# Reciprocals spread over partitions by four transfers of 32 source partitions each, in place of sixteen of one source partition each

## The chip, the cores and the metric

The kernel runs on one core of a Trainium2 chip. The metric is the device time of one execution in microseconds, as the median of a few runs. A core has five instruction streams that work side by side and wait for each other by semaphores: PE (matrix multiplications), DVE (vector work), ACT (activations and copies), POOL (a second vector engine) and SP, which here only issues transfers (DMAs). The transfers themselves are moved by 16 DMA engines.

## The reference, cut to what matters

The input x has 32 images of 256 channels and 32 x 32 = 1024 positions. Each image is group-normalised (32 groups of 8 channels), goes through a strictly causal attention with 8 heads of 32 channels, and is added to the result:

```python
def reference(x, q_w, q_b, kv_w, kv_b):
    xf = gn(x).reshape(B, C, S)                  # B=32, C=256, S=1024
    q = einsum('oc,bcs->bos', q_w, xf) + q_b
    kv = einsum('oc,bcs->bos', kv_w, xf) + kv_b  # k, v: 256 channels each
    # 8 heads of 32 channels
    scores = einsum('bhqd,bhkd->bhqk', q, k) / sqrt(32)
    attn = softmax(where(tril(ones, -1) == 0, -10000, scores))
    attn = where(tril(ones, -1) == 0, 0, attn)
    out = einsum('bhqk,bhkd->bhqd', attn, v)
    return x + out                               # all in float32
```

## The kernel before, in words

**Tiling.** An image lies in SBUF as 128 partitions x 2 groups x 1024 positions: channel c is partition c mod 128 of group g = c // 128, so a group holds four heads (j = 0 to 3) of 32 partitions. The attention of an image is 24 steps: two groups g, two halves hf of 512 query positions, and 4 or 8 blocks k of 128 keys. A step multiplies keys with queries for four heads (line 215, tile sT), takes exponentials on ACT (line 220, tile e), masks the diagonal block on POOL (line 225), and two steps later multiplies with the values (line 243, tile acc) while DVE adds the exponentials up over the key blocks (line 248).

**Denominators.** When a pair n = 2g + hf is through, `sums` (line 260, tile pd) reduces the summed exponentials over the key partitions with a matrix that puts the sum for head j of the pair n into the partitions 32j + n, 32j + n + 4, ..., eight copies each. `den` collects the four pairs: partition p of `den` holds 512 sums of head p // 32 and pair p mod 4. `invert` (line 279) takes the reciprocals of `den` in four pieces of 128 columns, tile rec.

**Spread and finish.** The final product needs each reciprocal on all 32 partitions of its head. `spread` (line 281) does that by DMAs from rec to a tile rb of 128 x 2 x 1024, which SP issues. `finish` (line 293) is called four times per image, once per pair n: DVE multiplies the numerators with the pair's 512 columns of rb (line 297), POOL adds x (line 298) and copies the first column of x (line 300), and after each second pair SP stores a group of the image (line 302).

**What sets the order.** PE, ACT, DVE and POOL run in the order in which the code emits instructions. A table `at` says in which step what is emitted beside the attention steps: the projections of the next image (lines 176 and 191, tiles pp and ppv), the norm of the image after that (lines 135 to 163), and, four steps into the next image and later, the denominators' check, the four pieces of `invert`, then `spread`, and the four `finish` calls five to eight steps behind `spread`. SP issues its DMAs in the order of the code as well. All matmuls of the projections, the norm's matmuls (pm, pv) and pd write through one single PSUM buffer, "misc", so each waits until the one before has been read by ACT or DVE. Each DMA carries one of eight semaphore lanes in turn (DMAHW0 to DMAHW7), and a DMA whose lane is in use first waits for that lane's last DMA.

**Names.** b is the image. v (line 196) is the evacuation of ppv by DVE, rstd (lines 155 and 156) that of pv, xn (line 163) the normalised image, num (line 252) the numerators.

Of the kernel before, what the change touches and what calls it, by code (L numbers as in the profile page):

```python
# [17 lines left out]
P = 128  # L18
HD = 32
CPG = 8  # L20
HALF = 512
# [9 lines left out]
def tile_norm_attention_residual(  # L31
# [19 lines left out]
    nc = tc.nc  # L51
# [4 lines left out]
    NH = S // HALF  # L56
# [18 lines left out]
    for n in range(4):  # L75
# [5 lines left out]
        out=avg, in_=avg, pattern=[[-CPG, P // CPG], [0, CPG]],  # L81
# [3 lines left out]
        out=avg, in_=avg, pattern=[[CPG, P // CPG], [0, CPG]],  # L85
# [24 lines left out]
    def unshifted():  # L110
# [170 lines left out]
        def spread(b):  # L281
            rec = live.pop(("rec", b))
            rb = work.tile([P, NG, S], F32, tag="rb", name=f"rb_{b}")
            for j in range(4):
                for n in range(4):
                    src = rec[HD * j + n : HD * j + n + 1, :]
                    nc.sync.dma_start(  # L287
                        out=rb[HD * j : HD * (j + 1), n // NH, (n % NH) * HALF : (n % NH + 1) * HALF],
                        in_=src.unsqueeze(1).broadcast_to([1, HD, HALF]),
                    )  # L290
            live["rb", b] = rb

        def finish(b, n):
# [25 lines left out]
        for b in range(B):  # L319
            if b + 2 < B:  # L320
                when(b * N, lambda b=b: load(b + 2))
                for n, f in zip((4, 6, 10, 14, 16, 18), prepare(b + 2)):
                    when(b * N + n, f)
            if b + 1 < B:
                for n, f in enumerate(projections(b + 1)):
                    when(b * N + 2 * n + 1, f)
            for s, (g, hf, k) in enumerate(per):
                if k == (hf + 1) * BPH - 1:
                    when(b * N + s + LAG + 2 + (s + LAG) % 2, lambda b=b, g=g, hf=hf: sums(b, g, hf))
            end = (b + 1) * N + LAG + 2  # L330
            when(end, lambda b=b: check_sums(b))
            for c in range(BPH):
                when(end + 1 + c, lambda b=b, c=c: invert(b, c))
            when(end + BPH, lambda b=b: spread(b))
            for n in range(4):
                when(end + BPH + 5 + n, lambda b=b, n=n: finish(b, n))
# [174 lines left out]
```

## Time and profile before

| | us |
|---|---|
| median of 3 runs | 2982.25 (2981.96 to 2987.22) |
| profiled execution, its own time | 2987.61 |
| its span, first to last instruction | 2985.9 |
| PE busy (matmuls) | 2317.2 (78%) |
| DVE busy | 1671.4 (56%) |
| ACT busy | 1386.7 (46%) |
| POOL busy | 960.5 (32%) |
| mean granted PE clock (1 is full speed) | 0.886 |

PE, DVE, ACT and POOL work side by side, so their busy times overlap and none alone is the span. Of a group of instructions the page gives busy time, the mean of one, and the idle time of the engine just before them with what ended most of it. The chain is the work that ended last, followed back in time. A transfer has two times: how long SP was occupied with issuing it, and the time from issue to landing.

### The profile page before, as it was taken

To read this page: it belongs to the slowest core of one execution; us is meant where nothing else is said; L and a number is where in the kernel's file an instruction comes from. 1 tells how busy PE (TensorE), PEld (TensorE's weight loads), DVE (VectorE), ACT (ScalarE), POOL (GpSimd) and SP (SyncE) were. 2 spreads that over 40 slices of the span, in tenths; PEclk is the share of its full clock that TensorE was granted. 3 is DMA by queue.
4 is the path that set the end of the run, shared out by engine and by line. 5 is a ranking of instruction groups with operands and counts; after the bars stand their busy time and mean duration, and the time that the engine had idled before them with its cause. 6 is when DMAs were issued, how large, how long until landed. Compare 5 with 4: busy or idle time off the path is not lost.

```text
span 2985.9 us, 38251 instructions
## 1 busy us (share of the span) xinstructions
PE 2317.2 (78%) x15502; PEld 860.3 (29%) x15502; DVE 1671.4 (56%) x1641; ACT 1386.7 (46%) x1921; POOL 960.5 (32%) x817
## 2 busy tenths in 40 slices
PE   5977798777897777887777977778977779877762
PEld 2322232222232222332222322222322223222320
DVE  2655565455575555664555655555645556555553
ACT  2644454444554444554444544445544445444441
POOL 1332333323242323233322324232333233333242
PEclk9988898888998888998889988889988889888885
DMA  1055433454433554334554335543335543344444
GB/s 69 1 43 43 14 38 36 41 43 24 32 37 37 43 43 22 32 37 40 43 43 14 37 37 43 43 22 33 36 39 43 43 15 38 36 41 29 29 22 36
DMA packets 44183, 104.14 MB, mean 35 GB/s; under 512 B 10336, under 2 KB 11232, under 8 KB 44000
## 3 DMA queue, kind: packets, MB, share of 16 engines
q1 hardware_dynamic: 44000, 101.62, 40.7%
q8 instruction: 124, 2.03, 0.3%
q14 instruction: 59, 0.48, 0.0%
HBM read 34.47 MB, written 33.55 MB: 23 GB/s over the span
## 4 chain that ended last, share of the span: by engine, by line
PE 47%; SPq 23%; DVE 13%; DMA 12%; issue 3%; ACT 1%; POOL 0%; DVEq 0%; POOLq 0%
SPq L287 23%; PE sT L215 14%; PE pp L176 13%; PE acc L243 12%; DMA rb<-rec 12%; DVE e L248 4%; PE ppv L191 4%; PE pd L260 3%; DVE rec L279 3%; DVE st L135 2%; DVE v L196 1%; DVE in_range L272 1%; DVE den L268 1%; DVE in_range L273 1%; PE pv L153 1%
## 5 line engine op out<-in xcount | busy, mean ns | idle before, releaser
L220 ACT ACTIVATE e<-sT 128x1024 f32<-128x1024 f32 (+3 forms) x1536 | 1148.7, 811 | 1310.9 <-PE sT L215 1029.2
L248 DVE TENSOR_TENSOR e<-e,e 128x2048 f32<-128x2048 f32 (+3 forms) x640 | 1126.5, 1760 | 242.9 <-PE acc L243 147.2
L225 POOL TENSOR_SCALAR_AFFINE_SELECT e<-e 128x512 f32<-128x512 f32 x512 | 714.8, 1405 | 1293.1 <-ACT e L220 1287.9
L215 PE MATMUL sT<-q,k 32*128 32x512 f32 (+3 forms) x6144 | 821.6, 541 | 0.5 <-ACT e L220 0.5
L243 PE MATMUL acc<-e,v 128*32 128x512 f32 (+3 forms) x6144 | 679.0, 515 | 19.2 <-ACT num L252 11.3
L176 PE MATMUL pp<-xn,wT 128*128 128x512 f32 x1024 | 509.5, 620 | 5.7 <-ACT q L180 3.1
L297 DVE TENSOR_TENSOR rb<-num,rb 128x512 f32<-128x512 f32 x128 | 90.4, 707 | 689.7 <-DMA rb<-rec 689.7
L215 PEld LDWEIGHTS sT<-q,k 32*128 32x128 f32 x6144 | 294.5, 188 | 557.2 <-issue 301.8
L153 PE MATMUL pv<-dev,avg 128*128 128x2 f32 x64 | 18.6, 360 | 532.5 <-DVE v L196 530.9
L298 POOL TENSOR_TENSOR rb<-rb,x 128x512 f32<-128x512 f32 x128 | 178.8, 1397 | 694.4 <-DVE rb L297 693.8
L191 PE MATMUL ppv<-wT,xn 128*128 128x256 f32 x1024 | 289.5, 431 | 17.8 <-DVE v L196 17.0
L243 PEld LDWEIGHTS acc<-e,v 128*32 128x32 f32 x6144 | 136.4, 110 | 458.0 <-issue 359.7
L176 PEld LDWEIGHTS pp<-xn,wT 128*128 128x128 f32 x1024 | 173.9, 189 | 270.2 <-issue 206.9
L191 PEld LDWEIGHTS ppv<-wT,xn 128*128 128x128 f32 x1024 | 207.5, 214 | 92.3 <-issue 40.3
L268 DVE TENSOR_TENSOR den<-den,pd 128x512 f32<-128x512 f32 x96 | 65.8, 685 | 218.4 <-PE pd L260 218.4
L153 PEld LDWEIGHTS pv<-dev,avg 128*128 128x128 f32 x64 | 15.8, 307 | 544.7 <-DVE v L196 542.8
L260 PE MATMUL pd<-e,pick 128*32 128x512 f32 x1024 | 138.1, 612 | 19.8 <-DVE e L248 19.8
L196 DVE TENSOR_TENSOR v<-ppv,v_bias 128x512 f32<-128x512 f32 x128 | 88.0, 688 | 104.4 <-PE ppv L191 104.4
L180 ACT ACTIVATE q<-pp,qk_bias 128x512 f32<-128x512 f32 x128 | 88.0, 688 | 112.8 <-PE pp L176 109.9
L180 ACT ACTIVATE k<-pp,qk_bias 128x512 f32<-128x512 f32 x128 | 88.2, 689 | 76.5 <-PE pp L176 74.2
L279 DVE RECIPROCAL rec<-den 128x128 f32<-128x128 f32 x128 | 118.6, 930 | 0.0
L252 ACT COPY num<-acc 128x512 f32<-128x512 f32 x128 | 74.3, 580 | 36.0 <-PE acc L243 36.0
(40 smaller groups left out, 371.1 us busy)
## 6 DMA issues: line engine op xcount, KB each, us to landing
x<-in_x_dram SPq DMA_DIRECT2D x32, 1024.0 KB, 5.9
rb<-rec SPq DMA_DIRECT2D x512, 64.0 KB, 10.7
out_dram<-rb SPq DMA_DIRECT2D x64, 512.0 KB, 2.9
wn<-in_L_conv_kv_w_dram SPq DMA_DIRECT2D x2, 256.0 KB, 3.5
wn<-in_L_conv_q_w_dram SPq DMA_DIRECT2D x1, 256.0 KB, 2.9
v_bias<-in_L_conv_kv_b_dram SPq DMA_DIRECT2D x1, 128.0 KB, 3.4
qk_bias<-in_L_conv_q_b_dram SPq DMA_DIRECT2D x1, 1.0 KB, 3.5
qk_bias<-in_L_conv_kv_b_dram SPq DMA_DIRECT2D x1, 1.0 KB, 3.2
```

What stands on the lines that cost most here:

```text
L176: nc.tensor.matmul(pp, lhsT=wT[:, cc, n * C + g * P : n * C + (g + 1) * P], rhs=live["xn", b][:, cc, cols], start=cc == 0, stop=cc == NG - 1,)
L180: nc.scalar.activation(live[key][:, cols], pp, AF.Identity, bias=qk_bias[:, n, g : g + 1], scale=(SCALE, 1.0)[n],)
L191: nc.tensor.matmul(pp[:, s, :], lhsT=live["xn", b][:, cc, (2 * n + s) * P : (2 * n + s + 1) * P], rhs=wT[:, cc, 2 * C : 3 * C], start=cc = ...
L215: nc.tensor.matmul(pairs[j // 2][:, j % 2, c0:], lhsT=kk[rows, k * P : (k + 1) * P], rhs=q[rows, hf * HALF + c0 : (hf + 1) * HALF], start= ...
L220: nc.scalar.activation(e[:, 2 * a : 2 * a + 2, c0:], pairs[a][:, :, c0:], AF.Exp)
L225: nc.gpsimd.affine_select(out=diagonal, in_=diagonal, pattern=[[0, 4], [1, P]], compare_op=ALU.is_gt, fill=0.0, base=0, channel_multiplier=-1,
L243: nc.tensor.matmul(acc[HD * j : HD * (j + 1), c0:], lhsT=live["v", b][:, k, h * HD : (h + 1) * HD], rhs=e[:, j, c0:], start=k == 0, stop=k ...
L248: nc.vector.tensor_add(total[:, :, c0:], total[:, :, c0:], e[:, :, c0:])
L260: nc.tensor.matmul(pd[HD * j : HD * (j + 1), :], lhsT=pick[:, n, :], rhs=total[:, j, :], start=True, stop=True, skip_group_check=True,)
L279: nc.vector.reciprocal(live["rec", b][:, cols], live["den", b][:, cols])
L287: nc.sync.dma_start(out=rb[HD * j : HD * (j + 1), n // NH, (n % NH) * HALF : (n % NH + 1) * HALF], in_=src.unsqueeze(1).broadcast_to([1, H ...
L298: nc.gpsimd.tensor_add(rb[:, g, cols], rb[:, g, cols], xt[:, g, cols])
```

## The change: four transfers with 32 source partitions each

```diff
         def spread(b):
             rec = live.pop(("rec", b))
             rb = work.tile([P, NG, S], F32, tag="rb", name=f"rb_{b}")
-            for j in range(4):
-                for n in range(4):
-                    src = rec[HD * j + n : HD * j + n + 1, :]
-                    nc.sync.dma_start(
-                        out=rb[HD * j : HD * (j + 1), n // NH, (n % NH) * HALF : (n % NH + 1) * HALF],
-                        in_=src.unsqueeze(1).broadcast_to([1, HD, HALF]),
-                    )
+
+            for n in range(4):
+                g, hf = divmod(n, NH)
+                nc.sync.dma_start(
+                    out=rb[:, g, hf * HALF : (hf + 1) * HALF],
+                    in_=rec[n::4, :].unsqueeze(1).broadcast_to([P // 4, 4, HALF]),
+                )
             live["rb", b] = rb
```

Before, transfer (j, n) reads one partition, 32j + n, 32 times and writes the 32 partitions of head j: 64 KB. Now, transfer n reads the 32 partitions n, n + 4, n + 8, ..., each four times, and writes all 128 partitions: 256 KB. The eight copies per head that `sums` makes are all used now; before, one of them was. The bytes per image (1 MB) and the size of one contiguous piece (2 KB) are the same.

On SP, at the spread of image 0 (rb_892 is its rb, rec_829 its reciprocals, DMAHW a lane that must be free), before:

```order
L128 DMA x_731<-in_x_dram 128x2x1024
L287 DMA rb_892<-rec_829 32x1x512 [waits DVE_49]
L287 DMA rb_892<-rec_829 32x1x512 [waits DMAHW3_49]
...
L287 DMA rb_892<-rec_829 32x1x512 [waits DMAHW1_49]
L302 DMA out_dram<-rb_892 128x1024 [waits DMAHW6_49,DMAHW3_49,DMAHW7_49,DMAHW2_49,Pool_49]
L302 DMA out_dram<-rb_892 128x1024 [waits DMAHW4_49,DMAHW1_49,DMAHW5_49,DMAHW0_49,Pool_49]
L128 DMA x_1239<-in_x_dram 128x2x1024
```

and now:

```order
L287 DMA rb_892<-rec_829 128x1x512 [waits DVE_49]
L287 DMA rb_892<-rec_829 128x1x512 [waits DMAHW3_49]
L287 DMA rb_892<-rec_829 128x1x512 [waits DMAHW4_49]
L287 DMA rb_892<-rec_829 128x1x512 [waits DMAHW5_49]
L302 DMA out_dram<-rb_892 128x1024 [waits DMAHW6_49,Pool_49]
L302 DMA out_dram<-rb_892 128x1024 [waits DMAHW7_49,Pool_49]
L128 DMA x_1227<-in_x_dram 128x2x1024 [waits DMAHW0_49]
```

Sixteen transfers took each of the eight lanes twice, so the later eight waited for the earlier eight of the same spread; four transfers take four lanes, which were last used by transfers of the image before.

On DVE, from the last additions before the first `finish` of image 0 to the normalisation behind the fourth (the numbers behind the names aside, the sequence of instructions is the same in both), before:

```order
L248 TENSOR_TENSOR e_1_0_1_0_793<-e_1_0_1_0_793,e_0_1_6_943 128x4x256 [waits DVE_49,Pool_49]
L297 TENSOR_TENSOR rb_892<-num_365,rb_892 128x512 [waits DMAHW6_49,DMAHW2_49]
L196 TENSOR_TENSOR v_931<-ppv_2_1016,v_bias 128x512 [waits PE_49]
L248 TENSOR_TENSOR e_1_0_1_0_793<-e_1_0_1_0_793,e_0_1_7_966 128x4x128 [waits DVE_49,Pool_49]
L297 TENSOR_TENSOR rb_892<-num_365,rb_892 128x512 [waits DMAHW7_49,DMAHW3_49]
L155 TENSOR_SCALAR rstd_1043<-pv_1041 128x2 [waits PE_49]
L297 TENSOR_TENSOR rb_892<-num_365,rb_892 128x512 [waits DMAHW4_49,DMAHW0_49]
L196 TENSOR_TENSOR v_931<-ppv_3_1064,v_bias 128x512 [waits PE_49]
L248 TENSOR_TENSOR e_1_1_0_0_987<-e_1_1_0_0_987,e_1_0_1_1003 128x4x384 [waits Pool_49]
L297 TENSOR_TENSOR rb_892<-num_365,rb_892 128x512 [waits DMAHW5_49,DMAHW1_49]
L163 TENSOR_SCALAR xn_1087<-x_731,mean_955,rstd_1043 128x1024 [waits Pool_49]
```

and now:

```order
L248 TENSOR_TENSOR e_1_0_1_0_793<-e_1_0_1_0_793,e_0_1_6_931 128x4x256 [waits DVE_49,Pool_49]
L297 TENSOR_TENSOR rb_892<-num_365,rb_892 128x512 [waits DMAHW2_49]
L196 TENSOR_TENSOR v_919<-ppv_2_1004,v_bias 128x512 [waits PE_49]
L248 TENSOR_TENSOR e_1_0_1_0_793<-e_1_0_1_0_793,e_0_1_7_954 128x4x128 [waits DVE_49,Pool_49]
L297 TENSOR_TENSOR rb_892<-num_365,rb_892 128x512 [waits DMAHW3_49]
L155 TENSOR_SCALAR rstd_1031<-pv_1029 128x2 [waits PE_49]
L297 TENSOR_TENSOR rb_892<-num_365,rb_892 128x512 [waits DMAHW4_49]
L196 TENSOR_TENSOR v_919<-ppv_3_1052,v_bias 128x512 [waits PE_49]
L248 TENSOR_TENSOR e_1_1_0_0_975<-e_1_1_0_0_975,e_1_0_1_991 128x4x384 [waits Pool_49]
L297 TENSOR_TENSOR rb_892<-num_365,rb_892 128x512 [waits DMAHW5_49]
L163 TENSOR_SCALAR xn_1075<-x_731,mean_943,rstd_1031 128x1024 [waits Pool_49]
```

No instruction of DVE moved. What differs is for what a `finish` waits: before, the pair n = 0 needed the transfers (j, 0) of all four heads, the last of which is the 13th that SP issues; now it needs the first of four.

## Rows read from the trace of the kernel before

**Rows 1.** Page, costliest groups: busy, mean ns | idle before, releaser.

```profile
L297 DVE TENSOR_TENSOR rb<-num,rb 128x512 f32<-128x512 f32 x128 | 90.4, 707 | 689.7 <-DMA rb<-rec 689.7
L153 PE MATMUL pv<-dev,avg 128*128 128x2 f32 x64 | 18.6, 360 | 532.5 <-DVE v L196 530.9
```

**Rows 2.** Chain that ended last, one image's spread: start us, us, what.

```profile
1062.89 0.51 SPq L287
...
1068.45 2.36 SPq L287
...
1084.81 11.34 DMA rb<-rec
```

**Rows 3.** Timeline of DVE, same image: start us, us, instruction, idle before, releaser.

```profile
1073.72 3.08 DVE L248 TENSOR_TENSOR e<-e,e 128x1536 f32<-128x1536 f32 x2
1096.24 0.69 DVE L297 TENSOR_TENSOR rb<-num,rb 128x512 f32<-128x512 f32 x1 [19.45 <-DMA rb<-rec]
...
1097.45 1.38 DVE L248 TENSOR_TENSOR e<-e,e 128x512 f32<-128x512 f32 x1
...
1105.76 0.68 DVE L297 TENSOR_TENSOR rb<-num,rb 128x512 f32<-128x512 f32 x1
```

**Rows 4.** Timeline of PE, same image: the matmul behind DVE's wait.

```profile
1097.59 0.59 PE L153 MATMUL pv<-dev,avg 128*128 128x2 f32 x2 [18.35 <-DVE v L196]
```

**Rows 5.** Stretches: A:B, us, busy of PE, PEld, DVE, ACT, POOL, clock, DMA, GB/s.

```profile
60.00:169.00 109.00, 108.18 (x736) 40.38 (x734) 69.30 (x69) 68.44 (x94) 34.26 (x31) 1.00 0.12 5
83.34:153.26 69.92, 69.57 (x488) 25.58 (x484) 47.91 (x47) 43.29 (x60) 22.56 (x19) 1.00 0.00 1
1062.43:1152.69 90.26, 71.57 (x488) 26.44 (x484) 52.13 (x52) 43.30 (x60) 31.13 (x25) 0.89 0.42 36
1097.00:1104.00 7.00, 6.41 (x38) 3.27 (x38) 3.91 (x7) 0.66 (x2) 6.92 (x7) 0.65 0.54 91
```

**Rows 6.** Timeline of PE in image 0, which has no finish in it.

```profile
101.82 1.99 PE L191 MATMUL ppv<-wT,xn 128*128 128x256 f32 x8
```

**Rows 7.** Timeline of DVE in image 0.

```profile
94.63 3.08 DVE L248 TENSOR_TENSOR e<-e,e 128x1536 f32<-128x1536 f32 x2
...
99.80 0.68 DVE L248 TENSOR_TENSOR e<-e,e 128x512 f32<-128x512 f32 x1
100.50 0.16 DVE L155 TENSOR_SCALAR rstd<-pv 128x2 f32<-128x2 f32 x1
```

**Rows 8.** Line 287, all 512 transfers of the spreads.

```profile
DMA to landing us min/median/max: 4.5/10.7/11.5
```

**Rows 9.** Page, DMA packets; issues: KB each, median us from issue to landing.

```profile
DMA packets 44183, 104.14 MB, mean 35 GB/s; under 512 B 10336, under 2 KB 11232, under 8 KB 44000
...
x<-in_x_dram SPq DMA_DIRECT2D x32, 1024.0 KB, 5.9
...
out_dram<-rb SPq DMA_DIRECT2D x64, 512.0 KB, 2.9
```

**Rows 10.** Timeline of SP: spreads of images 0, 29, 30 and 31.

```profile
153.73 31.67 SPq L287 DMA_DIRECT2D rb<-rec  x16
...
2785.06 31.69 SPq L287 DMA_DIRECT2D rb<-rec  x16
...
2868.39 31.81 SPq L287 DMA_DIRECT2D rb<-rec  x16
...
2937.08 31.95 SPq L287 DMA_DIRECT2D rb<-rec  x16
```

**Rows 11.** Timeline of PE at the finish of images 29 and 30.

```profile
2819.67 3.78 PE L191 MATMUL ppv<-wT,xn 128*128 128x256 f32 x8 [14.63 <-DVE v L196]
...
2903.18 1.93 PE L260 MATMUL pd<-e,pick 128*32 128x512 f32 x8 [18.53 <-DVE e L248]
```

**Rows 12.** Timeline, end of the run: first multiplication, last addition of image 31.

```profile
2970.57 0.69 DVE L297 TENSOR_TENSOR rb<-num,rb 128x512 f32<-128x512 f32 x1 [33.52 <-DMA rb<-rec]
...
2978.29 1.26 POOL L298 TENSOR_TENSOR rb<-rb,x 128x512 f32<-128x512 f32 x1
```

## The prediction

> **What bounds the kernel now.** I read the costliest groups first. There DVE stands idle for 689.7 us in front of the product of `finish`, released by the spread's transfers, and PE stands idle for 532.5 us in front of pv, released by DVE's v [rows 1]. The reader is to see one wait that is passed on, not two.
>
> The chain and the timelines of one image show how. SP begins to issue the spread at 1062.89. The middle issues occupy it for 2.36 us each (2.40 with the gap of 0.04 from one to the next), so the 13th leaves only at 1084.81 and lands 11.34 us later [rows 2]. DVE has finished its additions at 1073.72 + 3.08 = 1076.80, which is 13.91 us after the first issue, and then stands for 19.45 us in front of the first `finish`; v, which frees the one "misc" buffer, is queued behind it [rows 3]. So PE cannot start pv and stands for 18.35 us [rows 4]. When it resumes, its granted clock is 0.65 in the mean of the next 7 us, a mix of the levels 1.2 and 2.4 GHz, where without the pause it is 1.00 [rows 5].
>
> The stretches give the price, and also the case without the stall: image 0 has no `finish` in it. From one pd to the same pd an image later it takes 69.92 us, of which PE is busy 69.57; the image in the middle of the run takes 90.26, with PE busy 71.57 [rows 5]. The 20.34 between them is 18.35 of idle PE and 2.00 of matmuls at the lower clock. Without the stall PE is the bound, with nothing left over.
>
> **The change part by part.** *Issues.* Twelve of sixteen issues go. The four left need no lane of their own spread, so SP has no reason to wait between them except for a queue that is full, which I come to.
>
> *Landing.* Transfer n must land by the time that DVE reaches `finish` n: 13.9 us after the first issue for n = 0, and, placed in image 0's timeline by the step it stands in, about 17, 18 and 23 us for the others. What such a transfer takes is not in the trace: 256 KB from SBUF to SBUF, out of 32 partitions, each read four times. The nearest rows are a load of 1024 KB at 5.9 us from issue to landing and a store of 512 KB at 2.9 [rows 9]; the whole spread moves 1 MB, so by these it lands some 6 to 8 us after its first issue. That is the low end, and a gain below it is worth nothing, since it is hidden anyway. The high end is the rate of before, 64 KB in 2.40 us, hence 9.6 us for 256 KB. Of the shortest landing of before, 4.5 us [rows 8], 2.1 are then beside the 2.40. With T us per transfer the landings are at 2.1 + T, 2.1 + 2T, and so on: all four are hidden if T stays under about 5 (4T + 2.1 < 23). I take T at about 1.5, nearer to the load, because before all 16 engines read the same single partition, and now 32 are read at once. Up to T = 5 the sum does not depend on it.
>
> The 27 GB/s of before (64 KB in 2.40 us) are the rate of one source partition in the rows. The Trainium skill, page "SBUF — State Buffer", section "Door 1: The DMA port swizzle (why `[64,N]` ≈ `[32,N]`)", gives a reason: a transfer runs at the number of SBUF ports that its partitions reach times 27.2 GB/s, and every fourth partition reaches all sixteen. By it T would be an estimated 0.6 us; by the rows' high end 9.6. The trace agrees with the figure for one port; no run so far shows several.
>
> *What remains of `finish`.* Its four multiplications on DVE and its additions and copies on POOL stay. They no longer run while PE stands but beside PE's full work, and this is a cost. DVE is busy 52.13 of 90.26 us [rows 5], so it has some 17 us of air in 69.92. The tight place is rstd, which must free "misc" before PE's next ppv. In image 0 rstd runs at 100.50 to 100.66 and that ppv starts at 101.82 [rows 6, 7]: 1.16 us of slack. The first multiplication falls into the gap after 97.71 (94.63 + 3.08) and costs nothing. The second adds 0.69 ahead of rstd, and the addition of 128 x 512 ahead of it took 1.38 beside a POOL addition [rows 3] where it takes 0.68 alone [rows 7], so 0.70 more. 0.69 + 0.70 - 1.16 leaves 0.23 of waiting PE; I take 0.25 per image. The bounds: not below -0.35 (69.92 - 69.57, PE's own work), and not above the four POOL additions of 1.26 each [rows 12] laid end to end in DVE's way, 5.0.
>
> That upper bound is also what a rule would make of it. The Trainium skill, page "SBUF — State Buffer", section "Who interferes with whom", says that a DVE instruction with two SBUF inputs and a GpSimd instruction that reads SBUF exclude each other, whichever is second standing until the first is through. It speaks against this change, as DVE's additions and POOL's now meet in PE's full stretch; the doubled 128 x 512 addition agrees with it. By the rule with PE waiting for all of it the sum would be 29 x 4.8 = 138 us higher; by the slack in the rows nearly all of it is hidden.
>
> *The sum*, against the profiled execution. Its spreads start at 153.73, 2785.06, 2868.39 and 2937.08 (images 0, 29, 30, 31) and its span is 2985.9 [rows 10].
> - To the first spread nothing changes: 153.7.
> - 29 periods to image 29's spread, 2631.3 now (90.74 each); then 29 x (69.92 + 0.25) = 2034.9.
> - Image 30 brings no norm with it: 83.3 now, less 14.63 of idle PE [rows 11] and 2.0 of low clock: 66.7.
> - Image 31 brings no projections either: 68.7 now, less 18.53 [rows 11] and 2.0: 48.2.
> - The end, 48.8 now: 33.5 from the first issue to the first multiplication at 2970.57, 9.0 to the end of the last addition (2978.29 + 1.26), 6.4 for the last store [rows 12]. The first becomes about 3.5 (0.5 of issue, 3 of landing), the second 6.5 (0.7, four additions of 1.26, two copies), the third stays: 16.4.
>
> Together 2319.9 of span. The execution took 1.7 us more than its span (2987.61 against 2985.9), hence 2321.6; the median shown is 0.18% below the profiled execution, hence **2318 us**, 22% less than before.
>
> **The rivals.**
>
> *The rate of before stays (T = 9.6).* If a packet's time belongs to the DMA engine and not to the one source partition, 1 MB takes the 38.4 us it takes now. For it: the bytes and the 2 KB pieces are the same. Against it: the load moves 1 MB in 5.9 us with the same engines [rows 9]. Then the first `finish` is free (11.7 < 13.9), but the second, third and fourth wait, for landings at 21.3, 30.9 and 40.5 us. The fourth now runs 42.87 us after the first issue (1105.76 - 1062.89) [rows 3]; 2.4 are gained per image, 31 times: about 2907 us.
>
> *PE's clock does not hold.* Without the pauses PE runs 2200 us on end, and the trace shows the clock at 1.00 for 109 us in a row at most [rows 5]. Were the mean to be the 0.89 of the middle stretch all the same, a period would be 69.92 / 0.89 = 78.6, 8.6 more, and the time about 2580. Against it: the low clock stands only behind pauses.
>
> *Slower: the transfers use fewer engines.* The place is the same wait in front of `finish`, the price grows with T, and it decides from T = 10.2 us (4T + 2.1 = 42.9), 256 KB at under 26 GB/s. If the source's stride put a transfer on eight of the sixteen engines at the packet time of before, T were 19.2, the last landing 78.9 us after the first issue, 36 later than the fourth `finish` now, and the time about 2985 + 31 x 36 = 4100. Against it: the 10336 packets under 512 B are some sixteen for each issue [rows 9], so all engines take part in transfers of 32, 64 or 128 partitions, and 32 source partitions share out evenly.
>
> **How the numbers follow.** The forecast has 0.83, the rate of before 0.06, the clock 0.06, slower 0.03; 0.02 is for a T between 5 and 9.6. The forecast's own range is 2300 (29 x -0.6 below) to 2456 (the upper bound of the meeting on POOL), but its upper part is unlikely, since it needs DVE's air to be of no use. I give 2298 to 2410, which leaves the rivals out. A measurement of this kernel tells 0.2% (6 us) from no change. All but the last rival are faster by far: 0.95; within 0.2% can only be a T close to 10.2: 0.02; slower 0.03.
>
> **What would show it.** In the profile after, the wait of line 297 for rb should be gone from the groups but for the end of the run (about 3 us), and pv's wait for v with it. A period from pd to pd should be 70 to 70.5 us, the granted clock near 1.00 throughout, issues of line 287 about 0.5 us each, and landings under 6 us. The forecast fails if an issue still occupies SP for over 2 us, if landings come near 10 us or more, if the clock falls in stretches without a pause, or if the period is over 72 us because rstd or v come late behind the additions that meet POOL.

## The result: 2334.6 us, 22% less

The changed kernel takes 2334.61 us (median of 4 runs, 2330.79 to 2336.60) against 2984.43 us (4 runs, 2981.96 to 2987.22): a ratio of 0.7821, with a 95% interval of 0.7807 to 0.7834. The forecast was 2318 with a range of 2298 to 2410.

In the profile after, the wait that rows 1 show is gone. These are the groups of the page that answer to it, and three that grew (columns as in [rows 1]):

```profile
L176 PE MATMUL pp<-xn,wT 128*128 128x512 f32 x1024 | 513.3, 624 | 26.4 <-DVE den L268 20.7
...
L298 POOL TENSOR_TENSOR rb<-rb,x 128x512 f32<-128x512 f32 x128 | 209.2, 1634 | 13.0 <-DVE rb L297 12.6
...
L297 DVE TENSOR_TENSOR rb<-num,rb 128x512 f32<-128x512 f32 x128 | 135.3, 1061 | 2.4 <-DMA rb<-rec 2.4
...
L163 DVE TENSOR_SCALAR xn<-x,mean,rstd 128x1024 f32<-128x1024 f32 x64 | 68.6, 1074 | 1.6 <-POOL rstd L156 1.6
```

The 689.7 us that DVE stood in front of line 297 are 2.4, all of it at the end of the run, and pv's row with its 532.5 us of idle PE is no longer among the costliest. In its place, small, is a wait that was not there: 20.7 us of PE in front of pp, for den. And what DVE and POOL do in `finish` and beside it takes longer: 1061 ns for a multiplication where it was 707 [rows 1].

The transfers themselves, from the page after: the queue that carries them (packets, MB, share of 16 engines' time), and the issues as in [rows 9].

```profile
q1 hardware_dynamic: 37856, 101.60, 11.8%
...
rb<-rec SPq DMA_DIRECT2D x128, 256.0 KB, 2.5
```

A transfer of 256 KB lands 2.5 us after its issue, where one of 64 KB needed 10.7 in the median. The same megabytes occupy the DMA engines for 11.8% of the span, where it was 40.7%: most of the time that the packets took before was not needed to move their bytes. What held them up is for the experiments to show.

The stretches after, one period from pd to pd and nearly the whole run (columns as in [rows 5]):

```profile
1005.45:1076.09 70.64, 69.65 (x489) 25.61 (x485) 54.07 (x52) 43.29 (x60) 31.13 (x25) 1.00 0.13 46
60.00:2300.00 2240.00, 2202.12 (x15340) 806.16 (x15342) 1698.33 (x1584) 1375.49 (x1906) 981.23 (x788) 1.00 0.12 43
```

PE is busy for 69.65 of 70.64 us, and the granted clock is 1.00 in the mean of 2240 us, in which PE pauses only briefly (up to 2250 us never for more than 0.83 us). Against [rows 5] the period is 19.62 us shorter: 90.26 to 70.64.

### The profile page after: what moved, and what is told of

Same layout as the page of the kernel before. It is cut to its first block, busy times and chain, and to the rows that moved or that the text cites. A ratio compares the mean times of both kernels' runs of the same rounds, so it can differ in the third digit from the quotient of the medians.

```text
span 2334.8 us, 37671 instructions
## 1 busy us (share of the span) xinstructions
PE 2243.6 (96%) x15502; PEld 824.2 (35%) x15502; DVE 1735.7 (74%) x1641; ACT 1386.2 (59%) x1921; POOL 1001.5 (43%) x817
## 3 DMA queue, kind: packets, MB, share of 16 engines
q1 hardware_dynamic: 37856, 101.60, 11.8%
## 4 chain that ended last, share of the span: by engine, by line
PE 87%; DVE 8%; issue 2%; ACT 2%; POOL 1%; DMA 0%; SPq 0%; POOLq 0%; DVEq 0%
PE sT L215 27%; PE acc L243 23%; PE pp L176 21%; PE ppv L191 11%; PE pd L260 4%; DVE e L248 3%; DVE xn L163 2%; DVE v L196 1%; DVE den L268 1%; ACT num L252 1%; ACT q L180 1%; POOL e L225 1%; DVE rb L297 0%; PE pv L153 0%; PE pm L141 0%
## 5 line engine op out<-in xcount | busy, mean ns | idle before, releaser
L225 POOL TENSOR_SCALAR_AFFINE_SELECT e<-e 128x512 f32<-128x512 f32 x512 | 733.3, 1441 | 1284.7 <-ACT e L220 1284.7
L215 PE MATMUL sT<-q,k 32*128 32x512 f32 (+3 forms) x6144 | 811.7, 534 | 0.5 <-ACT e L220 0.5
L243 PE MATMUL acc<-e,v 128*32 128x512 f32 (+3 forms) x6144 | 652.8, 497 | 20.0 <-ACT num L252 11.3
L176 PE MATMUL pp<-xn,wT 128*128 128x512 f32 x1024 | 513.3, 624 | 26.4 <-DVE den L268 20.7
L215 PEld LDWEIGHTS sT<-q,k 32*128 32x128 f32 x6144 | 288.0, 183 | 532.6 <-issue 277.6
L191 PE MATMUL ppv<-wT,xn 128*128 128x256 f32 x1024 | 255.2, 392 | 3.1 <-DVE v L196 2.3
L298 POOL TENSOR_TENSOR rb<-rb,x 128x512 f32<-128x512 f32 x128 | 209.2, 1634 | 13.0 <-DVE rb L297 12.6
L191 PEld LDWEIGHTS ppv<-wT,xn 128*128 128x128 f32 x1024 | 184.1, 190 | 66.2 <-issue 33.8
L297 DVE TENSOR_TENSOR rb<-num,rb 128x512 f32<-128x512 f32 x128 | 135.3, 1061 | 2.4 <-DMA rb<-rec 2.4
L135 DVE BATCH_NORM_STATS2 st<-x 128x6 f32<-128x512 f32 x128 | 80.1, 668 | 4.7 <-DMA x<-in_x_dram 4.7
L163 DVE TENSOR_SCALAR xn<-x,mean,rstd 128x1024 f32<-128x1024 f32 x64 | 68.6, 1074 | 1.6 <-POOL rstd L156 1.6
```

The source lines that it names most:

```text
L176: nc.tensor.matmul(pp, lhsT=wT[:, cc, n * C + g * P : n * C + (g + 1) * P], rhs=live["xn", b][:, cc, cols], start=cc == 0, stop=cc == NG - 1,)
L191: nc.tensor.matmul(pp[:, s, :], lhsT=live["xn", b][:, cc, (2 * n + s) * P : (2 * n + s + 1) * P], rhs=wT[:, cc, 2 * C : 3 * C], start=cc = ...
L215: nc.tensor.matmul(pairs[j // 2][:, j % 2, c0:], lhsT=kk[rows, k * P : (k + 1) * P], rhs=q[rows, hf * HALF + c0 : (hf + 1) * HALF], start= ...
L225: nc.gpsimd.affine_select(out=diagonal, in_=diagonal, pattern=[[0, 4], [1, P]], compare_op=ALU.is_gt, fill=0.0, base=0, channel_multiplier=-1,
L243: nc.tensor.matmul(acc[HD * j : HD * (j + 1), c0:], lhsT=live["v", b][:, k, h * HD : (h + 1) * HD], rhs=e[:, j, c0:], start=k == 0, stop=k ...
L297: nc.vector.tensor_mul(rb[:, g, cols], num[:, g, cols], rb[:, g, cols])
```

## The experiments

Three questions were left: whether the number of transfers or their sources made the spread slow, what exactly a source shares with another, and where the 0.7 us come from by which the period is longer than the 69.92 of an image without `finish`. A theory that has a letter is explained in the expectation that names it first.

**Sixteen transfers of eight source partitions each.** The number of transfers stays, their sources change.

```diff
-                    src = rec[HD * j + n : HD * j + n + 1, :]
+                    src = rec[HD * j + n : HD * (j + 1) : 4, :]
...
-                        in_=src.unsqueeze(1).broadcast_to([1, HD, HALF]),
+                        in_=src.unsqueeze(1).broadcast_to([HD // 4, 4, HALF]),
```

> Sixteen transfers of 64 KB as before, in the order of before, but each reads 8 partitions (32j + n + 4m) four times instead of one partition 32 times. Theory A (one source partition delivers 64 KB in 2.40 us, and that alone made the spread slow): the 13th transfer leaves about 7 to 8 us after the first (0.6 us per issue) and lands by 11 us, under the 13.9 us at which DVE comes for it; about 2335 us, as with four transfers, issues of line 287 about 0.6 us each. Theory B (what cost was the number of transfers, 2.40 us for each with its lane and its completion): the spread stays at 38 us and the time at about 2985 us.

Measured: 2343.0 us, ratio 0.7854 (0.7832 to 0.7877). The timeline of SP shows one spread (start us, us):

```profile
1004.84 11.59 SPq L288 DMA_DIRECT2D rb<-rec  x16
```

Sixteen issues in 11.59 us instead of 31.7, 0.68 us each, although each lane is still taken twice. So theory B falls: the number of transfers costs little here (2343.0 against 2334.6 us), the source is what counted.

**The two loops swapped, sources as before.**

```diff
-            for j in range(4):
-                for n in range(4):
+            for n in range(4):
+                for j in range(4):
```

> The kernel before with the two loops of the spread swapped: the same sixteen transfers of one source partition, but the four of a pair n follow each other, so that the first finish needs the 4th transfer and not the 13th. Theory A (the rate of one source partition, transfer after transfer): landings of the four pairs at 11.7, 21.3, 30.9 and 40.5 us after the first issue; the first finish is free, the others wait in turn, the fourth at 40.5 instead of 42.9 us: about 2907 us. Theory C (the gain of the change is that a finish waits for the first transfer and no longer for the 13th): about 2335 us. If transfers from different partitions overlap, something between, with issues of less than 2.36 us.

Measured: 2468.7 us, ratio 0.8276 (0.8224 to 0.8327): neither 2907 nor 2335. From the chain of one image, the last issue and the landing behind it, with the spread's first issue (start us, us, what):

```profile
1053.40 0.51 SPq L287
...
1072.08 0.61 SPq L287
...
1072.74 6.56 DMA rb<-rec
```

The last transfer lands at 1079.30, 25.9 us after the first issue, where theory A had 40.5. The rate of one source partition is therefore not a toll on each transfer in turn: with the loops swapped, some transfers run beside each other. Which ones, this run does not tell; the run with heads 1 and 3 shifted does, further on. Swapping the loops brings about 514 of the 650 us, but it changes two things at once: which transfer the first `finish` waits for (theory C), and which sources are read side by side. This run does not part the two. The next one keeps the old order, in which the first `finish` needs the 13th transfer, and is nearly as fast as the change, so the gain does not need theory C.

**Another copy for each transfer.** Sixteen transfers in the order of before, one source partition each, but a different one of the eight copies.

```diff
-                    src = rec[HD * j + n : HD * j + n + 1, :]
+                    p = HD * j + n + 4 * ((4 * j + n) % 8)
+                    src = rec[p : p + 1, :]
```

> Sixteen transfers in the order of before, each still out of one single partition, but out of another of the eight copies: partition 32j + n + 4m with m = (4j + n) mod 8, so that no two transfers that follow each other read from the same four neighbouring partitions. If the limit of 2.40 us per 64 KB belongs to a transfer with one source partition, whichever partitions its neighbours in the queue read: 2985 us, issues of 2.36 us. If it belongs to the source partition (or the few beside it) and the engines go on to the next transfer while others still read: the spread shortens towards the 6 to 8 us of the changed kernel, and the time goes down to about 2335 us. The trace of before does not tell these apart, since there one transfer's neighbours read the neighbouring partition.

Measured: 2347.9 us, ratio 0.7871 (0.7848 to 0.7894). Its spread in the timeline of SP, and, of the line of the issues, the times from issue to landing:

```profile
1003.00 12.27 SPq L288 DMA_DIRECT2D rb<-rec  x16
```

```profile
DMA to landing us min/median/max: 3.9/4.1/5.3
```

This is the run that settles it: one source partition 32 times over, sixteen times, in the order of before, comes within 0.6% of the change (2347.9 against 2334.6 us), if the next transfer reads elsewhere. Each transfer alone still needs 4.1 us where 256 KB of the change land in 2.5, but several are on their way together. Each lane is taken twice here as well, so the lanes did not make the spread of before slow.

**The loops swapped, heads 1 and 3 four partitions further on.** Does the gain come from two partitions 32 apart no longer sharing?

```diff
-            for j in range(4):
-                for n in range(4):
-                    src = rec[HD * j + n : HD * j + n + 1, :]
+            for n in range(4):
+                for j in range(4):
+                    p = HD * j + n + 4 * (j % 2)
+                    src = rec[p : p + 1, :]
```

> The kernel before with sixteen transfers of one source partition, grouped by pair n as in the run with the loops swapped, but for the heads 1 and 3 out of the copy four partitions further on: the four transfers of a pair read partitions n, 36 + n, 64 + n, 100 + n instead of n, 32 + n, 64 + n, 96 + n. With the loops swapped alone the sixteen took 21 us to issue (1.25 us each in the median). If partitions 32 apart share what delivers 27 GB/s (two such groups were at work there, 1 MB in 19 us), four groups are now at work: 10 to 12 us for sixteen issues, the last landing about 14 us after the first issue instead of 26, and no wait of DVE for rb: about 2340 us. If instead at most two transfers overlap, whatever they read: 21 us of issues and about 2469 us as before.

Measured: 2347.6 us, ratio 0.7866 (0.7850 to 0.7882). In the timeline of SP:

```profile
1005.46 12.58 SPq L288 DMA_DIRECT2D rb<-rec  x16
```

A shift by four partitions for half of the transfers takes the sixteen issues from 21.07 to 12.58 us. So n and 36 + n do not share what delivers 27 GB/s; nor do n and 64 + n, since both are still read here side by side. By [rows 2] neighbours such as 0, 1, 2 and 3 share it. That n shares it with 32 + n is not told by this run alone, since the shift parts n from 96 + n too. The trace of before bears it out: there the landings of a spread follow each other 2.41 us apart (median of 32 spreads), and also where the sources pass from partition 3 to partition 32. But the eighth, the last one ahead of partition 64, lands 1.78 us after the seventh, and the sixteenth, the last of all, 0.47 us after the fifteenth. The sixteenth has no transfer behind it; that the eighth comes early too, and the fourth does not, fits a group that ends ahead of 64 and none that ends ahead of 32. The Trainium skill, page "SBUF — State Buffer", section "Door 1: The DMA port swizzle (why `[64,N]` ≈ `[32,N]`)", has just this table: partitions 0 to 3 and 32 to 35 on one port, 64 to 67 on another, 4 to 7 on a third. These runs agree with it (2.41 us from landing to landing on one port, 12.58 us for sixteen issues on four). A section further on, "Can I just issue two DMAs to hit both halves?", the same page of the Trainium skill says that two transfers, one on a tile at partition 0 and one on a tile at partition 64, serialize, with a gain of 6% only; by these runs transfers of one queue that each read a single partition overlap as soon as their ports differ (12.58 us against 31.7), and the measurement decides.

**Four transfers of four source partitions.** The count of the change, with the sources of before.

```diff
-                    in_=rec[n::4, :].unsqueeze(1).broadcast_to([P // 4, 4, HALF]),
+                    in_=rec[n::HD, :].unsqueeze(1).broadcast_to([4, HD, HALF]),
```

> Four transfers of 256 KB as in the change, but each reads only the four partitions n, n + 32, n + 64, n + 96, 32 times each. Theory A: 64 KB out of each source partition, so 2.40 us per transfer if the four partitions deliver side by side, 4.8 us if two of them share, so landings of the last at about 12 or 21 us after the first issue; both are under the 23 us at which DVE comes for the fourth, and the time is about 2335 us either way, with longer landings than the 2.5 us of the change in the profile. Theory B (number of transfers): like the changed kernel, landings of 2.5 us too. Over 2400 us would say that the four transfers take more than 5 us each.

Measured: 2384.6 us, ratio 0.7994 (0.7970 to 0.8017). From the chain (start us, us, what), and from the timelines of DVE and PE:

```profile
1013.13 0.55 SPq L287
...
1016.58 20.77 DMA rb<-rec
```

```profile
1037.38 0.69 DVE L297 TENSOR_TENSOR rb<-num,rb 128x512 f32<-128x512 f32 x1 [1.35 <-DMA rb<-rec]
```

```profile
1039.45 3.53 PE L176 MATMUL pp<-xn,wT 128*128 128x512 f32 x4 [1.18 <-DVE den L268]
```

The fourth transfer lands 24.2 us after the first issue; by 2.1 + 4T that is T = 5.5, and DVE waits 1.35 us for it. Theory B falls once more (landings are not 2.5 us), and theory A's own number was too kind: 4.8 us was expected, and no wait. It costs some 50 us against the changed kernel, 1.6 per image, some of it because PE's pause of 1.18 us is followed by matmuls at the lower clock: this pp takes 3.53 us instead of 1.98, at a granted clock of 0.55 in the mean from 1039.4 to 1043.0. Of the 29 pauses in front of this pp, 1.16 to 1.91 us long, 9 were followed by such a slow pp (3.51 to 3.78 us); behind the other 20 it took 1.98 or 1.99. Their length does not tell the two apart: 1.18 us was followed by either.

**What is left above 69.92: the last finish one step later, or xn one step later.** Two separate kernels, run beside the changed one again (2336.05 us, 2334.87 to 2338.05; ratio 0.7829, 0.7815 to 0.7842).

> The changed kernel itself, for the comparison with the two beside it: 2331 to 2337 us, as in its four runs so far, with a wait of about 0.65 us per image of PE's pp for den.

```diff
-                when(end + BPH + 5 + n, lambda b=b, n=n: finish(b, n))
+                when(end + BPH + 5 + n + n // 3, lambda b=b, n=n: finish(b, n))
```

> The changed kernel with the fourth finish of an image one step later, behind the addition of pd into den instead of ahead of it. Theory D (what is left above the period without a finish, some 0.7 us per image, is the chain v, e, finish, xn, den on DVE, stretched where it meets POOL's additions, in front of PE's pp): without the finish in that chain den comes 1.1 us earlier, pp no longer waits, the period is 69.9 to 70.0 us instead of 70.6, and the time falls by 28 to 30 x 0.65, about 20 us, to about 2315 us. Rival E (the excess is the amount of DVE and POOL work that came into PE's full stretch, wherever it stands): the wait comes back at the next evacuation, 2331 to 2337 us.

```diff
-                for n, f in zip((4, 6, 10, 14, 16, 18), prepare(b + 2)):
+                for n, f in zip((4, 6, 10, 14, 17, 18), prepare(b + 2)):
```

> The changed kernel with the first half of the normalisation (xn) of an image one step later, behind the addition of pd into den, and the finish where it was. Theory D: xn with its 1.75 us beside POOL's addition leaves the chain in front of den, which comes earlier by that; same gain as for the finish put later, about 2315 us. Rival E: 2331 to 2337 us. If only the finish put later helps and this does not, the finish itself and not the length of the chain is what delays den.

Measured: 2316.01 us (2315.49 to 2317.17), ratio 0.7761 (0.7748 to 0.7774), and 2316.12 us (2311.14 to 2318.92), ratio 0.7764 (0.7751 to 0.7777). The chain that they cut, from the timeline of DVE in the changed kernel:

```profile
1016.74 3.08 DVE L248 TENSOR_TENSOR e<-e,e 128x1536 f32<-128x1536 f32 x2
1019.73 1.12 DVE L297 TENSOR_TENSOR rb<-num,rb 128x512 f32<-128x512 f32 x1
...
1021.91 1.27 DVE L248 TENSOR_TENSOR e<-e,e 128x512 f32<-128x512 f32 x1
...
1023.71 0.15 DVE L155 TENSOR_SCALAR rstd<-pv 128x2 f32<-128x2 f32 x1
...
1025.97 0.69 DVE L196 TENSOR_TENSOR v<-ppv,v_bias 128x512 f32<-128x512 f32 x1 [1.15 <-PE ppv L191]
1026.58 1.75 DVE L248 TENSOR_TENSOR e<-e,e 128x1536 f32<-128x1536 f32 x1
1028.24 1.12 DVE L297 TENSOR_TENSOR rb<-num,rb 128x512 f32<-128x512 f32 x1
1029.29 1.75 DVE L163 TENSOR_SCALAR xn<-x,mean,rstd 128x1024 f32<-128x1024 f32 x1
1030.97 0.67 DVE L268 TENSOR_TENSOR den<-den,pd 128x512 f32<-128x512 f32 x1
```

and of PE in the same stretch:

```profile
1023.94 1.99 PE L191 MATMUL ppv<-wT,xn 128*128 128x256 f32 x8
...
1031.69 1.98 PE L176 MATMUL pp<-xn,wT 128*128 128x512 f32 x4 [0.65 <-DVE den L268]
```

From v at 1025.97 DVE does not stand still until den is through at 1031.64, and PE, ready for pp 0.65 us earlier, waits for it because den's source holds the "misc" buffer. In 18 of the 29 periods this wait is 0.65 us, in 11 it is 0.82. POOL's mask (line 225) and additions (line 298) run meanwhile:

```profile
1026.58 2.25 POOL L225 TENSOR_SCALAR_AFFINE_SELECT e<-e 128x512 f32<-128x512 f32 x1
1028.80 1.70 POOL L298 TENSOR_TENSOR rb<-rb,x 128x512 f32<-128x512 f32 x1
```

They stretch the chain: the multiplication takes 1.12 us and xn 1.75, where they take 0.69 and 0.81 by themselves. The multiplication ends at 1029.36, 0.53 us behind the mask (1028.83), and xn at 1031.04, 0.54 behind the addition (1030.50). It is so in the whole run: all 112 multiplications (line 297) and normalisations (line 163) of the changed kernel that take longer than by themselves end 0.53 to 0.56 us behind a mask or an addition of POOL. So DVE is held until POOL's instruction is through. With the last `finish` behind den, the same stretch is

```profile
1014.50 0.69 DVE L196 TENSOR_TENSOR v<-ppv,v_bias 128x512 f32<-128x512 f32 x1 [1.15 <-PE ppv L191]
1015.11 2.24 DVE L248 TENSOR_TENSOR e<-e,e 128x1536 f32<-128x1536 f32 x1
1017.27 1.76 DVE L163 TENSOR_SCALAR xn<-x,mean,rstd 128x1024 f32<-128x1024 f32 x1
1018.95 0.68 DVE L268 TENSOR_TENSOR den<-den,pd 128x512 f32<-128x512 f32 x1
```

Here den ends 1019.63 - 1014.50 = 5.13 us after v's start, where it took 5.67. That is 0.54 us earlier and not the 1.1 expected, because the addition in front of xn now takes 2.24 us instead of 1.75. The period is 70.09 us (1016.25 to 1086.34, from pd to pd), and the wait of pp for den is gone; the 0.17 left above 69.92 is not explained. Taking out xn goes a little further; then the period in the timeline of PE is the 69.92 of the image without `finish`, to the hundredth:

```profile
1016.83 1.06 PE L260 MATMUL pd<-e,pick 128*32 128x512 f32 x8
...
1086.75 1.07 PE L260 MATMUL pd<-e,pick 128*32 128x512 f32 x8
```

Theory D holds: 20 us by either cut, and no wait of that size comes back elsewhere (rival E). The medians of the two kernels do not differ (2316.01 and 2316.12), though their periods do by 0.17 us. These two are also the fastest of the kernels here.

## Why the prediction was right, and where its sum was off

**The wait and its price.** Right. The 18.35 us of idle PE and the 2.00 of low clock per image went together; the period fell by 19.62 in the image looked at.

**The landing.** Right in the forecast's sense: each transfer lands long before DVE comes (the fourth 4.4 us after the first issue, DVE 22.3), and T did not enter the sum. The reason given for it (one source partition against 32) was right in kind and too narrow: the copies in use lay on two of the places that deliver 27 GB/s, and the queue came to the second only after the first. The rival that the rate of before stays is out by the 2.5 us of landing. The limit "under about 5" stood up: DVE comes for the fourth transfer 22.3 us after the first issue (1028.24 - 1005.92), not 23, which by 4T + 2.1 makes T = 5.05, and in the run with T = 5.5 there is a wait of 1.35 us.

**The meeting of `finish` with POOL.** Here the place was wrong and the size too small. I had looked for it at rstd, with 1.16 us of slack, and taken 0.25 us per image. rstd ran at 1023.71 to 1023.86 in front of a ppv at 1023.94: just in time, no wait. The wait came one evacuation later, at den, 0.65 or 0.82 us, since a `finish`, a slower xn and den stand there behind one v. The period was 70.64 in the image looked at and 70.71 in the mean, not 70.17. The two bounds held it, and the fear that PE would wait for all four POOL additions did not come true.

**The clock.** The rival that it sinks in a long run without long pauses is out: 1.00 over 2240 us.

**Term by term.** From the timeline of SP in the profile after, the spreads of the images 0, 28, 29, 30 and 31:

```profile
157.37 3.58 SPq L287 DMA_DIRECT2D rb<-rec  x4
...
2137.21 2.48 SPq L287 DMA_DIRECT2D rb<-rec  x4
...
2205.55 3.01 SPq L287 DMA_DIRECT2D rb<-rec  x4
...
2271.40 2.49 SPq L287 DMA_DIRECT2D rb<-rec  x4
...
2320.87 2.48 SPq L287 DMA_DIRECT2D rb<-rec  x4
```

| term | forecast | measured |
|---|---|---|
| to the first spread | 153.7 | 157.4 |
| 29 periods | 2034.9 | 2048.2 |
| image 30 | 66.7 | 65.9 |
| image 31 | 48.2 | 49.5 |
| the end | 16.4 | 13.9 |
| span | 2319.9 | 2334.8 |

The 13.3 us of the periods are the largest mis-sized term, with 0.25 us of waiting at rstd forecast and 0.65 or 0.82 at den measured: 28 of them take 70.71 in the mean where 70.17 was forecast, which makes 15; the last takes only 68.34 and gives some back. The first term moved without the change: in this execution the first three groups of pp took 3.78 us each at the lower clock, where before it was only one group at 3.65; in the kernels here the first spread came between 153.3 and 157.4. The end was 2.5 us cheaper: 2.40 from the first issue to the first multiplication (2323.27), where I had taken 3.5; 7.4 from there to the end of the last addition (2330.68), where I had 6.5; and 4.1 for the last store, where I had kept the 6.4 of before. Why that store was shorter stays open. One more slip is in the last step: 0.18% off 2321.6 is 2317.4, where 2318 stands.

## What to carry to other kernels

A slow transfer can be slow because of what its neighbours in the queue read: before cutting their number, look which partitions those in flight share, and let successive transfers read from different ones. Ask by when each piece is needed, not how long the whole takes; here swapping two loops, which put the pieces in the order of their use and let two groups of partitions be read side by side, brought most of the gain. When a stall goes, the work that it covered meets the full stretch of the bound engine: look there at every evacuation that frees a shared buffer, and count what stands behind one another in front of it, each at its duration beside the other engine.

## What the runs showed of the hardware that was not expected

- Transfers of one queue overlap: sixteen that each read a single partition took 12.3 us to issue where no two shared a source group of partitions, 12.6 where four groups were at work, 21.1 where two were, and 31.7 where one was at a time.
- An issue on SP takes 0.5 to 0.7 us where nothing holds it. The 2.36 of before was a wait and not work: the same sixteen transfers of 64 KB out of other partitions have a median issue of 0.64 us.
- A lower clock does not follow each pause of PE: in the changed kernel pp took 1.98 us behind all 29 waits of 0.65 to 0.83 us for den; in the run with four source partitions, behind 29 pauses of 1.16 to 1.91 us, it took 3.5 to 3.8 us in 9 cases and 1.98 in 20.
- A multiplication or a normalisation on DVE that was held by POOL's mask or addition ended 0.53 to 0.56 us behind it, in all 112 cases of the changed kernel; so 0.69 us became 1.12, and 0.81 became 1.75.
